# Three elementwise steps of a two-layer graph network on GpSimd in place of VectorE

## The chip, the cores and the metric

The kernel runs on one core of one Trainium2 chip. A core has five engines with a queue each: TensorE (PE, matrix products into PSUM), VectorE (DVE) and ScalarE (ACT, elementwise work), GpSimd (POOL) and SyncE (SP, which here issues almost all DMAs). Each engine works through its own instructions in order and waits on semaphores of the others. The metric is the time of one execution on the device in microseconds; the median of four runs before is 2351.61 us (2350.25 to 2352.42).

## The reference

128 graphs of 128 nodes with 512 features pass through two layers, all in float32. In short:

```python
# x: [128, 128, 512], adj: [128, 128, 128]
h = maximum(layernorm(x), 0)                       # layer 0: a transformer
q, k, v = h @ Wq.T + bq, h @ Wk.T + bk, h @ Wv.T + bv     # 8 heads of 64
s = (q @ k.T) * 64 ** -0.5 * (adj + adj)
x = x + (softmax(s) @ v) @ Wo.T + bo
h = maximum(layernorm(x), 0)                       # layer 1: a graph attention
Wh = h @ W
e = leaky_relu(Wh @ a[:512] + (Wh @ a[512:]).T, 0.2)
att = softmax(where(adj > 0.5, e, -9e15), axis=1)
x = x + elu(att @ Wh)
```

## The kernel before

**Tiling.** The 128 graphs are taken two by two: 64 *pairs* p. Two pairs make a *group* g of four graphs, whose tokens share the q, k and v products. The nodes of a graph lie on the 128 partitions, so the residual x of a pair is a tile `xs[p]` of 128x1024 (two graphs, 512 features). The input transposed, features on partitions, is loaded as the tile `hA` of a group.

**Layer norm of layer 0.** Statistics are taken from rows of x (`stats0`, L165 and L166), the power -1/2 on GpSimd (`row_stats.power`, L172 and L173), and both numbers of each row go through DRAM (`spread0`, a DMA that GpSimd issues at L208; `fetch0`, issued by SP at L213) into a tile `mr` that has them along the free dimension. Then `hidden(p, 0)` (L222) subtracts the means from the pair's half of `hA` and `hidden(p, 1)` (L224) applies the maximum with 0 and multiplies by the scale. These steps are called `hd0` and `hd1`; they exist for pairs 4 to 63. The first four pairs are normalised by rows and turned over by TensorE.

**Products with seven in place of eight.** Each 512x512 product is cut into quarters and done with seven products of quarters (`PRODUCTS`), after sums of quarters have been formed. `token_sum` forms the four sums of an operand: for the hidden rows (`hidden_sum`, steps `hs0` to `hs3`, tile `hS`; the last, L157, overwrites a quarter of `hA`), for the context (`cs`, tile `cxT`) and for the gathered rows of layer 1 (`gs`, tile `gT`). Accumulators lie in eight PSUM banks (`ps1`); a bank is free again when ScalarE or VectorE has read it. The products of the output projection go into `row_a` and `row_c`, and `add0` (L402, steps `od`) adds them to `xs[p]`.

**The constant row.** The biases of v and of the output projection come to one row c that is the same for all tokens. `shift(p)` (L234, step `sh`) adds it to `xs[p]` before the first `od` step of the pair. `xs[p]` has three buffers and is loaded by SP at L72.

**Attention.** TensorE makes scores (L320), VectorE weighs them with the adjacency (L327, `at`) and takes maxima (L334), ScalarE exponentials (L339) and the division (L348). VectorE transposes 32x32 blocks (L355); two DMAs through DRAM place them (L359, L365). TensorE multiplies by v (L388). Layer 1 follows for the pair before: row statistics, `nmr` (L412), hidden rows on ScalarE (L418), dots with a on VectorE (L425), softmax, gathering (L481), the product with W, and the ELU (L511, L515).

**Order.** All of it is written out by hand: the lists `HEAD`, `ORDER` and `TAIL` name steps with the pair they work on, and the program issues them one after another, so that each engine's queue holds its share of them in this order. `ORDER` is one iteration of the steady part, run for p from 3 to 59; with its lags it works on pair p in attention, p-1 in the output projection, p-2 and p-3 in layer 1, and p+4 in the hidden rows. An odd iteration ends with `hs2` and `hs0` of the next group but one; the even iteration after it has `hs1` and `hs3`. GpSimd's queue holds, in each iteration, the power of layer 1 (L172, L173) and that of layer 0 with its DMA (L172, L173, L208).

Of the kernel before, what the change touches and what calls it, by code (L numbers as in the profile page):

```python
# [10 lines left out]
OP = mybir.AluOpType  # L11
AX = mybir.AxisListType

P = 128
# [10 lines left out]
def kernel(  # L25
# [18 lines left out]
    nc = tc.nc  # L44
    B, S, E = x.shape
# [14 lines left out]
    xs, x0s, adjs, adjTs, hAs, hSs = {}, {}, {}, {}, {}, {}  # L60
# [57 lines left out]
    c_sb, u_sb = const.tile([P, E], F32, name="c"), const.tile([P, 2, E], F32, name="u")  # L118
# [26 lines left out]
        else:  # L145
            nc.vector.tensor_tensor(w[:, 6], w[:, 2], w[:, 5], OP.subtract)

    def token_sum(h, s, k):

        if k == 0:  # L150
            nc.vector.tensor_tensor(s[:, 0], h[:, 2], h[:, 3], OP.add)
        elif k == 1:
            nc.vector.tensor_tensor(s[:, 1], s[:, 0], h[:, 0], OP.subtract)  # L153
        elif k == 2:
            nc.vector.tensor_tensor(s[:, 2], h[:, 0], h[:, 2], OP.subtract)
        else:
            nc.vector.tensor_tensor(h[:, 2], h[:, 1], s[:, 1], OP.subtract)  # L157

    def row_stats(src, name, soon=False):

# [56 lines left out]
    def hidden(p, k):  # L217

        h = hAs[p // 2][:, 2 * (p % 2) : 2 * (p % 2) + 2].rearrange("p q c k -> p (q c) k")
        row = rows0[p][:, None, :, k].to_broadcast([P, 2 * 2, 2 * S])  # L220
        if k == 0:
            nc.vector.tensor_tensor(h, h, row, OP.subtract)  # L222
        else:
            nc.vector.scalar_tensor_tensor(h, h, 0.0, row, op0=OP.max, op1=OP.mult)  # L224

    def hidden_sum(g, k):
        if g not in hSs:
            hSs[g] = grp.tile([P, 3, 2, 2 * S], F32, name="hS")
        token_sum(hAs[g], hSs[g], k)

    def shift(p):


        nc.vector.tensor_tensor(xs[p], xs[p], c_sb[:, None, :].to_broadcast([P, 2, E]), OP.add)  # L234

    accs = {}

# [442 lines left out]
    def steps(p):  # L680
# [21 lines left out]
        for k in range(4):  # L702
            table[f"cs{k}"] = lambda k=k: token_sum(cxT, cxT[:, 4:7], k)
            table[f"gs{k}"] = lambda k=k: token_sum(gTs[p], gTs[p][:, 4:7], k)
# [7 lines left out]
        for i in range(2):  # L712
# [9 lines left out]
            "pr": lambda: leaky1(p), "m1": lambda: maxima1(p), "e1": lambda: exps1(p), "sw": lambda: normalise1(p),  # L722
            "ez": lambda: elu(p), "fa": lambda: finish_a(p), "fb": lambda: finish_b(p), "so": lambda: store(p),
            "sh": lambda: shift(p),
        }
        if p < N - 2:
# [18 lines left out]
        if p + 4 < N:  # L745
            table |= {
                "f0": lambda: fetch0(p + 4), "lT": lambda: load_xT(p + 4),
                "hd0": lambda: hidden(p + 4, 0), "hd1": lambda: hidden(p + 4, 1),
            }
# [6 lines left out]
        if odd and (g + 2) * 2 < N:  # L756
            for k in range(4):
                table[f"hs{k}"] = lambda k=k: hidden_sum(g + 2, k)
# [70 lines left out]
```

## Time and profile before

| what | value |
|---|---|
| median of four runs | 2351.61 us |
| the profiled execution | 2352.27 us |
| its span, first to last instruction | 2350.5 us |
| mean granted TensorE clock | 0.997 |
| ScalarE busy | 1467.0 us, 62% |
| GpSimd busy | 256.5 us, 11%, 320 instructions |
| DMA queue of SP (q1) | 311.31 MB, 43.8% of 16 engines' span |

The profile is of one execution. Times in a timeline are microseconds from the span's start. A group of instructions is named by its line in the kernel, its engine, its operation, and out<-in by the program's names with partitions and elements; then come count, busy time, mean length in ns and the idle time of the engine just before, with what ended it. PEld is TensorE's loading of weights, which overlaps its products. A wait names who waited and who released it.

The longest waits of GpSimd and VectorE, in us in total, times, and longest:

```
POOL mv L172 <- DVE mv L166: 1998.0, 123, 34.1
DVE x L402 <- PE row_a L299: 137.1, 149, 2.0
DVE x L234 <- DMA x<-in_x: 40.1, 28, 2.6
DVE at L327 <- PE sc L320: 39.8, 60, 1.2
DVE nmr L412 <- POOL mv L173: 16.8, 28, 0.6
```

### The profile page before, as it was taken

The numbers are of one execution on the slowest core, as the hardware profiler recorded it, in microseconds if no ns is written. First come the engines' busy times: TensorE is split into PE (matmuls) and PEld (weight loads), VectorE is DVE, ScalarE is ACT, GpSimd is POOL, SyncE is SP. The second block draws the span as 40 slices with busy tenths as digits, with TensorE's granted clock in tenths as the row PEclk, the third lists the DMA queues.
The fourth block names the chain that finished last, engine by engine and source line by source line (L and its number), as shares of the span: only waits on it lengthen the run. The fifth ranks groups of instructions, "written<-read, shape, count | busy, mean of one in ns | idle before, by whom it ended". The sixth has DMA issues, their size and how long they took to land.

```text
span 2350.5 us, 41028 instructions
## 1 busy us (share of the span) xinstructions
PE 2336.3 (99%) x14184; PEld 2064.5 (88%) x14184; DVE 2001.5 (85%) x4113; ACT 1467.0 (62%) x4815; POOL 256.5 (11%) x320
## 2 busy tenths in 40 slices
PE   9999999999999999999999999999999999999998
PEld 8888888888888888888888888888888888888886
DVE  5888888888888888888888888888888888888888
ACT  2666566666566665666666666656666566666774
POOL 1101101111111011011110111110101101110000
PEclk8999999999999999999999999999999999999999
DMA  4445354454444544434445445444344443443332
GB/s 157 135 122 148 120 149 117 132 158 127 140 128 126 154 131 137 140 114 145 148 124 152 117 124 161 125 144 136 120 148 136 132 140 112 147 149 118 118 119 95
DMA packets 267351, 314.06 MB, mean 134 GB/s; under 512 B 24200, under 2 KB 192136, under 8 KB 267144
## 3 DMA queue, kind: packets, MB, share of 16 engines
q1 hardware_dynamic: 263112, 311.31, 43.8%
q8 instruction: 112, 1.84, 0.3%
q0 software_dynamic: 1920, 0.13, 0.2%
q14 instruction: 95, 0.78, 0.1%
q10 hardware_dynamic: 2112, 0.01, 0.0%
HBM read 210.51 MB, written 100.85 MB: 132 GB/s over the span
## 4 chain that ended last, share of the span: by engine, by line
PE 99%; DMA 0%; DVE 0%; ACT 0%; issue 0%; SPq 0%; DVEq 0%; ACTq 0%
PE acc_a L258 29%; PE row_a L299 23%; PE acc_c L258 14%; PE row_c L299 9%; PE acc_b L258 7%; PE sc L320 5%; PE pc L388 5%; PE pg L481 5%; DMA wq<-in_wqT 0%; PE pm L531 0%; DMA bq<-in_bq 0%; PE pt L197 0%; ACT z L495 0%; DVE x L402 0%; DVE st L165 0%
## 5 line engine op out<-in xcount | busy, mean ns | idle before, releaser
L339 ACT ACTIVATE at<-at,nmx 128x128 f32<-128x128 f32 x1024 | 396.2, 390 | 19.7 <-DVE nmx L334 17.9
L299 PE MATMUL row_a<-wo,cxT 128*128 128x256 f32 x1280 | 328.5, 379 | 0.3 <-DVE cxT L153 0.3
L348 ACT ACTIVATE at<-at,rs 128x128 f32<-128x128 f32 x1024 | 324.0, 392 | 5.8 <-DVE rs L343 5.7
L299 PE MATMUL row_a<-w,gT 128*128 128x256 f32 x1280 | 319.4, 380 | 2.9 <-DVE z L499 1.7
L172 POOL TENSOR_SCALAR mv<-mv 128x2 f32<-128x2 f32 x124 | 79.2, 638 | 2020.2 <-DVE mv L166 1998.0
L299 PEld LDWEIGHTS row_a<-w,gT 128*128 128x128 f32 x1280 | 242.3, 190 | 37.9 <-DVE z L499 2.6
L299 PEld LDWEIGHTS row_a<-wo,cxT 128*128 128x128 f32 x1280 | 242.6, 190 | 34.3 <-DVE cxT L153 0.6
L402 DVE TENSOR_TENSOR x<-row_a,x 128x256 f32<-128x256 f32 x320 | 135.1, 422 | 139.9 <-PE row_a L299 137.1
L495 ACT COPY z<-row_a 128x256 f32<-128x256 f32 x256 | 94.5, 369 | 210.4 <-PE row_a L299 210.2
L275 ACT ACTIVATE kT<-acc_a,bk 128x256 f32<-128x256 f32 x256 | 106.7, 467 | 171.4 <-PE acc_a L258 168.2
L327 DVE SCALAR_TENSOR_TENSOR at<-sc,adj 128x512 f32<-128x512 f32 x256 | 165.1, 686 | 42.2 <-PE sc L320 39.8
L339 ACT ACTIVATION_READ_ACCUMULATOR at<-at,nmx 128x1 f32 x1024 | 193.7, 189 | 0.0
L275 ACT ACTIVATE qT<-acc_a,bq 128x256 f32<-128x256 f32 x256 | 106.3, 467 | 123.1 <-PE acc_a L258 123.1
L165 DVE BATCH_NORM_STATS2 st<-x 128x6 f32<-128x512 f32 x256 | 176.1, 688 | 7.5 <-DMA x<-in_x 5.2
L425 DVE SCALAR_TENSOR_TENSOR junk<-h,u 128x512 f32<-128x512 f32 x256 | 173.4, 677 | 0.6
L355 DVE STREAM_TRANSPOSE tr<-at 128x1024 f32<-128x1024 f32 x128 | 158.9, 1241 | 9.3 <-PE pc L388 2.7
L334 DVE TENSOR_REDUCE nmx<-at 128x8 f32<-128x1024 f32 x128 | 156.2, 1220 | 4.3
L487 ACT COPY gT<-pg 128x512 f32<-128x512 f32 x128 | 74.7, 585 | 123.6 <-PE pg L481 117.4
L481 PEld LDWEIGHTS pg<-w,h 128*128 128x128 f32 x1024 | 133.3, 192 | 6.6 <-ACT z L495 0.2
L173 POOL TENSOR_TENSOR mv<-mv,mhalf 128x2 f32<-128x2 f32 x128 | 130.6, 1021 | 32.0 <-DVE mv L168 21.7
L481 PE MATMUL pg<-w,h 128*128 128x128 f32 x1024 | 134.1, 275 | 0.0
L299 PE MATMUL row_c<-w,gT 128*128 128x256 f32 x512 | 133.1, 382 | 0.6 <-DVE z L499 0.5
(130 smaller groups left out, 4884.9 us busy)
## 6 DMA issues: line engine op xcount, KB each, us to landing
blocks<-tr SPq DMA_DIRECT2D x128, 512.0 KB, 6.5
aT<-blocks SPq DMA_DIRECT2D x512, 128.0 KB, 2.9
x<-in_x SPq DMA_DIRECT2D x123, 512.0 KB, 5.2
out<-x SPq DMA_DIRECT2D x63, 512.0 KB, 4.1
hA<-in_xT SPq DMA_DIRECT2D x120, 256.0 KB, 3.6
mr<-rows SPq DMA_DIRECT2D x60, 256.0 KB, 4.2
adj<-in_adj SPq DMA_DIRECT2D x64, 128.0 KB, 3.9
adjT<-in_adjT SPq DMA_DIRECT2D x64, 128.0 KB, 3.7
```

Source lines behind the costliest of these rows:

```text
L165: nc.vector.bn_stats(st, src[:, i, :])
L258: nc.tensor.matmul(acc[:, m, :], lhsT, rhs, start=fresh and m == 0 and c == 0, stop=c == 1, skip_group_check=True)
L275: nc.scalar.activation(dst(t, f)[:, m, :], a[:, m, :], AF.Identity, bias=bias[:, j : j + 1])
L299: nc.tensor.matmul(acc, left[:, la, c, :], w[:, wb, c, :], start=n in (0, 3) and c == 0, stop=c == 1, skip_group_check=True)
L327: nc.vector.scalar_tensor_tensor(ats[b][0][:, k * C : (k + 1) * C, :], scs[b][k], QSCALE, adjs[p][:, i : i + 1, :].to_broadcast([P, C, S]) ...
L334: nc.vector.tensor_reduce(nmx, at, AX.X, OP.max, negate=True)
L339: nc.scalar.activation(at[:, j, :], at[:, j, :], AF.Exp, bias=nmx[:, j : j + 1], accum_out=sums[:, j : j + 1])
L348: nc.scalar.activation(at[:, j, :], at[:, j, :], AF.Copy, scale=rs[:, j : j + 1])
L355: nc.vector.transpose(trs[b], at.rearrange("p h (j k) -> p j h k", k=Q))
L402: nc.vector.tensor_tensor(d, row_acc(p, "o", bank), d, OP.add)
L425: nc.vector.scalar_tensor_tensor(junk, h2[:, i, :], 1.0, u_sb[:, k, :], op0=OP.mult, op1=OP.mult, accum_out=ws[:, i, 1:2] if k else src_sb ...
L481: nc.tensor.matmul(pg[:, c, :], h1s[p][0][:, i, c * P : (c + 1) * P], wts[p][:, i, :], start=True, stop=True)
```

## The change

`shift`, the first half of `hidden`, and `token_sum` for the hidden rows of the groups from 2 on are issued to GpSimd. The sums of the first two groups, of the context and of the gathered rows stay on VectorE. The lists of steps are not touched, so the moved instructions stand in GpSimd's queue where the lists have them, between the powers and the small DMAs.

```diff
-    def token_sum(h, s, k):
+    def token_sum(h, s, k, engine=nc.vector):
 
         if k == 0:
-            nc.vector.tensor_tensor(s[:, 0], h[:, 2], h[:, 3], OP.add)
+            engine.tensor_tensor(s[:, 0], h[:, 2], h[:, 3], OP.add)
         elif k == 1:
-            nc.vector.tensor_tensor(s[:, 1], s[:, 0], h[:, 0], OP.subtract)
+            engine.tensor_tensor(s[:, 1], s[:, 0], h[:, 0], OP.subtract)
         elif k == 2:
-            nc.vector.tensor_tensor(s[:, 2], h[:, 0], h[:, 2], OP.subtract)
+            engine.tensor_tensor(s[:, 2], h[:, 0], h[:, 2], OP.subtract)
         else:
-            nc.vector.tensor_tensor(h[:, 2], h[:, 1], s[:, 1], OP.subtract)
+            engine.tensor_tensor(h[:, 2], h[:, 1], s[:, 1], OP.subtract)
...
         if k == 0:
-            nc.vector.tensor_tensor(h, h, row, OP.subtract)
+            nc.gpsimd.tensor_tensor(h, h, row, OP.subtract)
         else:
...
-        token_sum(hAs[g], hSs[g], k)
+        token_sum(hAs[g], hSs[g], k, nc.gpsimd if g > 1 else nc.vector)
 
     def shift(p):
...
-        nc.vector.tensor_tensor(xs[p], xs[p], c_sb[:, None, :].to_broadcast([P, 2, E]), OP.add)
+        nc.gpsimd.tensor_tensor(xs[p], xs[p], c_sb[:, None, :].to_broadcast([P, 2, E]), OP.add)
```

## The prediction, made before the changed kernel was run

> **What bounds the kernel now.** I read the busy times of the page first, then the same by stretches of the span. The columns of a stretch are its length, then busy time and instructions of PE, PEld, DVE, ACT and POOL, the granted clock, the DMA share and GB/s.
>
> ```profile
> PE 2336.3 (99%) x14184; PEld 2064.5 (88%) x14184; DVE 2001.5 (85%) x4113; ACT 1467.0 (62%) x4815; POOL 256.5 (11%) x320
> 90.00:1000.00 910.00, 910.00 (x5541) 805.88 (x5540) 781.07 (x1598) 575.80 (x1900) 99.43 (x122) 1.00 0.45 134
> 1000.00:2260.00 1260.00, 1260.00 (x7721) 1116.72 (x7721) 1081.43 (x2216) 803.71 (x2651) 138.68 (x166) 1.00 0.44 133
> 2260.00:2351.00 91.00, 81.49 (x478) 67.56 (x474) 78.60 (x179) 50.89 (x151) 4.06 (x8) 1.00 0.32 105
> ```
>
> From 90 to 2260 us TensorE has no gap, at full clock. The chain of waits says the same: PE is 99% of it, and its groups return every 72.2 us (an x16 of acc_a at 1023.23, the next at 1095.45). So 233 us of VectorE work can be taken away there without gaining anything; a change can only open gaps. What counts is how late each step may come before PE stands still. I call that its room. 72.2 us are two pairs: an odd iteration (1002 to 1038) and an even one (1038 to 1074).
>
> **What is removed.** VectorE loses these (columns: count | busy us, mean ns | idle before):
>
> ```profile
> L234 DVE TENSOR_TENSOR x<-x,c 128x1024 f32<-128x1024 f32 x64 | 78.2, 1221 | 40.1 <-DMA x<-in_x 40.1
> L222 DVE TENSOR_TENSOR hA<-hA,mr 128x1024 f32<-128x1024 f32 x60 | 73.0, 1216 | 0.0
> L155 DVE TENSOR_TENSOR hS<-hA 128x512 f32<-128x512 f32 x32 | 22.1, 691 | 1.0
> L151 DVE TENSOR_TENSOR hS<-hA 128x512 f32<-128x512 f32 x32 | 21.9, 685 | 1.5 <-ACT hA L200 1.4
> ```
>
> With L153 and L157 (683 and 682 ns) and 30 of each sum moved (the first two groups stay): 78.2 + 73.0 + 30 x (0.691 + 0.685 + 0.683 + 0.682) = 233 us; VectorE falls to about 1768 us, 75%. Worth nothing by itself. No DMA moves, and the orders of PE, ACT and SP are the same.
>
> **What is added.** GpSimd gets 64 + 60 instructions of 1024 elements and 120 of 512. The trace has no elementwise instruction of such length there, so I bound it by its plain ones:
>
> ```profile
> masks.py:199 POOL TENSOR_SCALAR_AFFINE_SELECT ident<-ident 128x128 f32<-128x128 f32 x1 | 0.3, 283 | 0.0
> L371 POOL MEMSET src<- 128x64 f32 x1 | 0.2, 152 | 0.0
> L102 POOL MEMSET mhalf<- 128x1 f32 x1 | 0.1, 98 | 0.0
> ```
>
> Fixed cost 98 ns. Writing alone: (152 - 98)/63 = 0.86 ns an element. Reading one and writing: (283 - 98)/128 = 1.45. Lower end, a second input for nothing: 98 + 1024 x 1.45 = 1.58 us. Upper end, the second input as dear as another pass: 98 + 1024 x 2.9 = 3.07 us. I take one more stream at the write price, 2.31 ns: 2.46 us for 1024, 1.28 us for 512 (bounds 0.84 and 1.58). The sum on GpSimd is 124 x 2.46 + 120 x 1.28 = 459 us (bounds 297 and 570). Even if VectorE stood still through all of it, 1768 + 459 = 2227 us would fit into the span, so VectorE doesn't become the bound on average.
>
> The Trainium skill speaks against the change: GPSIMD Engine Reference, "Performance versus the Vector engine", calls elementwise work with two inputs about twice as slow there and gives 4497 ns against 2293 for 2048 elements. An estimate from that page is 2.25 us for 1024; the sum by it would be 124 x 2.25 + 120 x 1.12 = 413 us, and the rooms below would hold a little more easily.
>
> **What lies in the way of what.** The two engines get into each other's way (timeline: start, length, engine):
>
> ```profile
> 1004.83 1.20 DVE L511 SCALAR_TENSOR_TENSOR x<-z,x 128x1024 f32<-128x1024 f32 x1
> 1005.08 1.02 POOL L172 TENSOR_SCALAR mv<-mv 128x2 f32<-128x2 f32 x1 [22.98 <-DVE mv L166]
> 1016.20 0.30 POOL L172 TENSOR_SCALAR mv<-mv 128x2 f32<-128x2 f32 x1 [8.27 <-DVE mv L166]
> 1016.34 0.42 DVE L499 TENSOR_TENSOR z<-row_a,z 128x256 f32<-128x256 f32 x1
> 1016.58 0.70 POOL L173 TENSOR_TENSOR mv<-mv,mhalf 128x2 f32<-128x2 f32 x1
> ```
>
> L172 takes 0.30 us, but 1.02 when L511 (two inputs in SBUF) runs, and ends 0.07 us after it. L499, with one input in PSUM, leaves L173 at its 0.70. So a VectorE instruction with two SBUF inputs holds GpSimd back until it ends; one that reads PSUM does not. Whether GpSimd holds VectorE back the same way no row shows, for want of long instructions there. Bounds: nothing, or its whole length. I take the whole length, but only against VectorE's two-input instructions. The Trainium skill (SBUF — State Buffer, "SBUF: two separate sides") has it so: the shared port pair is an exclusive lock, and whoever starts first keeps it for the instruction. By it the blocking is the one I take; without it the forecast would lose about 1 us of its tail.
>
> **Shift, even iteration.** The tightest room:
>
> ```profile
> 1060.71 1.23 DVE L234 TENSOR_TENSOR x<-x,c 128x1024 f32<-128x1024 f32 x1 [1.15 <-DMA x<-in_x]
> 1062.47 0.87 DVE L402 TENSOR_TENSOR x<-row_a,x 128x256 f32<-128x256 f32 x2
> 1065.19 1.03 PE L299 MATMUL row_a<-wo,cxT 128*128 128x256 f32 x4
> ```
>
> It starts when x lands, so an early start on another engine wins nothing. On GpSimd it ends at 60.71 + 2.46 = 63.17, L402 twice by 64.1; PE needs that at 1065.0 (its weight load is 0.2 us ahead). 0.9 us are left, and at the upper bound of 3.07 still 0.3. VectorE has nothing with two SBUF inputs to do in that stretch. In two of the later periods (PE at 1859.55 and 2003.97) x landed late enough that VectorE ended only 0.6 and 0.8 us before PE; there PE loses about 0.6 us each: +1.2 us.
>
> **Shift and means, odd iteration.** x is issued at 1015.03, and the transfer is over by about 1018.2 (slices of 0.2 us from 1014, GB/s):
>
> ```profile
> GB/s 0 0 0 0 0 0 0 4 1 0 113 123 0 0 287 420 389 430 389 348 123 0 0 0 5 5 0 0 471 389 410 369 471 287 20 41 20 20 20 20
> 1018.77 1.29 DVE L327 SCALAR_TENSOR_TENSOR at<-sc,adj 128x512 f32<-128x512 f32 x2
> 1019.57 1.08 PE L299 MATMUL row_c<-w,gT 128*128 128x256 f32 x4
> PEld row_c L299 <- DVE at L327: 5.2, 28, 0.2
> ```
>
> GpSimd issues its small DMA until 1018.35, then shifts (18.4 to 20.9) and subtracts the means of a later pair at once (20.9 to 23.3), ten us ahead of before. Beside it VectorE runs L327, which frees a bank for PE with no room at all (the last line: PE waited for it 28 times), but reads PSUM. Then come a maximum (one input) and at 1021.23 four sums with two SBUF inputs, which stand until 1023.3: 2.1 us late, less the 1.2 us of the shift that they no longer wait for. L402 (room 3.3 us to PE at 1028.25) and L279 (3.5 us to 1029.98) come 0.9 us late, and VectorE's idle 2.0 us at 1027.3 takes that up. Nothing reaches PE.
>
> **Sums and the rest.** hs2 and hs0 follow L224 (ends 1036.59) until 1039.2. Queued behind them on GpSimd are the two instructions of the variance (L172 at 1041.09 before), still in time. hs1 follows those and may hold L412 until about 1044.3, against 1043.68 before; the scores that VectorE needs next come at 1044.27. hs1 ends near 1044.3 and PE reads it at 1053.11; hs3 queues behind the small DMA, ends near 1056 and is read at 1061.74. Cover is 5 to 9 us. The means of the even iteration (63.2 to 65.6) are due at 1072.31.
>
> **Head and tail.** The head's moved steps have VectorE consumers 8 us away or more. In the tail, where PE and VectorE alternate without room, the shift at 2299.22 can start earlier but holds three sums (+0.6), and the one at 2313.42 starts when x lands and ends 1.2 us later (+0.7 after an idle 0.4). Sum: 1.2 + 1.3 = +2.5 us.
>
> The profiled execution took 2352.27 us, 2350.5 of it the span; it lies 0.7 us above the median of 2351.61. 2352.27 + 2.5 = 2354.8, or 2354 against the median.
>
> **Rivals.**
> - *GpSimd is too slow (0.22).* Decides from about 3.3 us for 1024 elements: room of the even shift, 1.23 + the 0.4 us that L402 waited for something else + 1.64. Above it each us costs 1 in the even iteration, and from 3.5 us on 2 in the odd one, where shift and means stand in line ahead of the sums. At 4 us: (0.7 + 1.0) x 31 = 53 us, 2405; at 3.6 us 2368. For it: a pow of only two elements takes 0.70 us there, and L172 is stretched threefold by VectorE. Against: the rows of the plain instructions.
> - *GpSimd holds VectorE even where that reads PSUM (0.20).* Then the odd shift, from 18.4 to 20.9, stands on L327 at 1018.77, whose bank PE takes at 1019.57: up to 2.1 us a period, 31 x 2.1 = 65 us, 2417; half as much, 2384, where only one of the pair is caught. It decides as soon as the shift starts before 1018.8. Against: L173 beside L499.
> - *Faster (0.03).* PE's idle 2350.5 - 2336.3 = 14 us lies ahead of 90 and behind 2260; the tail could give back some 5 us if VectorE's lighter queue shortened its alternation: 2346.
> - *It does not do what it says*: excluded, the three lines stand on GpSimd in the built order, 244 of them.
>
> **How the numbers follow.** The forecast, no change to speak of, has 0.55, with a range of its own of 2349 to 2358. What a measurement of this kernel tells from no change is about 0.2%, 4.7 us, so up to 2356.3; of the 0.55 some 0.07 lie above. Same: 0.48. Slower: 0.07 + 0.22 + 0.20 = 0.49. Faster 0.03. The range reaches to 2402: it leaves out about 0.18 in all, most of it the far ends of the two slow rivals.
>
> **What would show it.** Right: the x<-x,c group on POOL at 2.2 to 2.8 us mean, PE without a gap from 90 to 2260, VectorE near 75%, its idle time larger, and the sums at 1021 waiting for POOL. Wrong: POOL means above 3.3 us, PE waits for L402 once in each even iteration, or for L327 in each odd one, longer than 0.2 us; or a period above 72.2 us.

## The result, and the profile after

The changed kernel takes 2354.86 us (median of 42 runs, 2351.37 to 2356.94) against 2351.51 us for the kernel before (60 runs, 2347.8 to 2353.01): a ratio of 1.0016, 95% interval 1.0012 to 1.002. It is about 3.4 us slower, less than the 4.7 us that the prediction took for the limit. The profiled execution took 2354.78 us, 2353.0 of it the span; before it was 2352.27 and 2350.5.

Busy times of the page of the changed kernel, then three stretches of its span (length, then busy us and instructions of PE, PEld, DVE, ACT and POOL, granted clock, DMA share, GB/s):

```profile
PE 2337.4 (99%) x14184; PEld 2064.3 (88%) x14184; DVE 1888.7 (80%) x3869; ACT 1472.5 (63%) x4815; POOL 726.3 (31%) x564
```

```profile
90.00:1000.00 910.00, 910.00 (x5541) 805.81 (x5540) 732.89 (x1494) 578.71 (x1903) 297.49 (x226) 1.00 0.45 134
1000.00:2260.00 1260.00, 1259.74 (x7698) 1115.88 (x7696) 1015.78 (x2079) 806.11 (x2648) 400.56 (x302) 1.00 0.45 133
2260.00:2353.00 93.00, 83.66 (x502) 69.18 (x501) 80.51 (x180) 52.01 (x156) 11.26 (x11) 1.00 0.32 105
```

VectorE has lost 244 instructions and 113 us of busy time, TensorE still has no gap from 90 to 1000 us and only 0.26 us of gaps from there to 2260. The 2.5 us of the span lie ahead of 90, in two spots of the long middle, and in the tail.

The moved groups, and two VectorE groups that were *not* touched by the diff (count | busy us, mean ns | idle before):

```profile
L234 POOL TENSOR_TENSOR x<-x,c 128x1024 f32<-128x1024 f32 x64 | 151.0, 2359 | 204.5 <-DMA x<-in_x 120.5 <-ACT v L270 59.4 <-issue 15.1
L222 POOL TENSOR_TENSOR hA<-hA,mr 128x1024 f32<-128x1024 f32 x60 | 145.0, 2416 | 17.0 <-DMA hA<-in_xT 17.0
...
L157 DVE TENSOR_TENSOR gT<-gT 128x256 f32<-128x256 f32 x64 | 75.3, 1177 | 0.1
...
L412 DVE SCALAR_TENSOR_TENSOR nmr<-mv 128x2 f32<-128x2 f32 x64 | 43.2, 674 | 34.6 <-POOL mv L173 34.6
...
L155 POOL TENSOR_TENSOR hS<-hA 128x512 f32<-128x512 f32 x30 | 38.3, 1277 | 377.5 <-DVE hA L224 377.5
L151 POOL TENSOR_TENSOR hS<-hA 128x512 f32<-128x512 f32 x30 | 38.1, 1269 | 14.9 <-DVE hA L224 14.9
```

The first two rows and the last two are the price: 2.36 and 2.42 us for 1024 elements, 1.26 to 1.29 us for 512. The middle two are the news. In the profile before the same groups were these:

```profile
L157 DVE TENSOR_TENSOR gT<-gT 128x256 f32<-128x256 f32 x64 | 26.6, 416 | 0.1
...
L412 DVE SCALAR_TENSOR_TENSOR nmr<-mv 128x2 f32<-128x2 f32 x64 | 10.0, 156 | 16.8 <-POOL mv L173 16.8
```

L412 handles two numbers a partition, yet its mean went from 156 to 674 ns. The timeline says how (start, length, engine). First an odd iteration of the changed kernel, then the even one after it:

```profile
1019.83 1.29 DVE L327 SCALAR_TENSOR_TENSOR at<-sc,adj 128x512 f32<-128x512 f32 x2
1019.96 2.35 POOL L234 TENSOR_TENSOR x<-x,c 128x1024 f32<-128x1024 f32 x1 [0.55 <-DMA x<-in_x]
...
1020.63 1.08 PE L299 MATMUL row_c<-w,gT 128*128 128x256 f32 x4
...
1022.28 2.39 POOL L222 TENSOR_TENSOR hA<-hA,mr 128x1024 f32<-128x1024 f32 x1
1022.29 2.65 DVE L157 TENSOR_TENSOR gT<-gT 128x256 f32<-128x256 f32 x1
...
1044.24 1.26 POOL L153 TENSOR_TENSOR hS<-hS,hA 128x512 f32<-128x512 f32 x1
1044.30 1.22 DVE L412 SCALAR_TENSOR_TENSOR nmr<-mv 128x2 f32<-128x2 f32 x1 [0.61 <-POOL mv L173]
...
1062.01 2.35 POOL L234 TENSOR_TENSOR x<-x,c 128x1024 f32<-128x1024 f32 x1 [5.30 <-DMA x<-in_x]
...
1064.39 0.88 DVE L402 TENSOR_TENSOR x<-row_a,x 128x256 f32<-128x256 f32 x2 [0.77 <-POOL x L234]
...
1066.26 1.03 PE L299 MATMUL row_a<-wo,cxT 128*128 128x256 f32 x4
```

L327 runs beside the shift in its usual 1.29 us, and PE takes its bank. L157, 0.42 us long before, is drawn out to 2.65 us: it starts with L222 and ends 0.27 us after it. L412 is drawn out to 1.22 us and ends 0.02 us after L153. So a held VectorE instruction doesn't show as idle time; its record is as long as the hold. The whole trace says the same: of the VectorE instructions that begin while a moved instruction runs on GpSimd with more than 0.3 us to go, all 63 with two inputs in SBUF are drawn out and end 0.01 to 0.55 us after it, and none of the 425 others, which have one input or read PSUM, is longer than before by as much as 0.1 us. The busy time of VectorE in the new page is its work and 103 us of standing still (what 64 records are longer than before), which makes the work about 1786 us. The prediction's 1768 took the moved records off in full, though neighbouring records overlap by a little under 0.1 us. In the even iteration the shift ends at 1064.36, L402 at 1065.27, and PE comes at 1066.26 with its weight load 0.2 us ahead: 0.8 us of room are left. Over 28 even iterations, from 195 to 2151 us, this room is 0.05 to 1.12 us and 0.66 on average, since x lands at a different time in each.

Three rows of the list of what TensorE itself waited for, in the changed kernel (us in total, times, longest):

```profile
PE acc_b L258 <- DVE at L327: 1.3, 1, 1.3
PE row_a L299 <- DVE cxT L153: 0.8, 1, 0.8
...
PE row_a L299 <- DVE x L402: 0.2, 1, 0.2
```

The first and the last did not stand in the list before, and the middle one stood there with 0.3 us. The first is in the head, where the chain led through a sum of weights (L144, 0.68 us long before, started at 61.48):

```profile
61.01 3.13 DVE L144 TENSOR_TENSOR wo<-wo 128x512 f32<-128x512 f32 x1
61.23 2.36 POOL L234 TENSOR_TENSOR x<-x,c 128x1024 f32<-128x1024 f32 x1
...
67.81 1.28 DVE L327 SCALAR_TENSOR_TENSOR at<-sc,adj 128x512 f32<-128x512 f32 x2
...
68.54 0.70 PE L258 MATMUL acc_b<-hA,wk 128*128 128x256 f32 x2 [1.27 <-DVE at L327]
```

The shift of pair 0 stood in VectorE's queue behind other work before and started at 70.18. On GpSimd's empty queue it starts nine microseconds sooner, and L144, which has two inputs in SBUF, stands still until it is over. L327 came at 65.82 before and comes at 67.81 now. Three lines of the profile before:

```profile
61.48 0.68 DVE L144 TENSOR_TENSOR wo<-wo 128x512 f32<-128x512 f32 x1
...
67.58 1.89 PE L258 MATMUL acc_b<-hA,wk 128*128 128x256 f32 x8
...
70.18 1.22 DVE L234 TENSOR_TENSOR x<-x,c 128x1024 f32<-128x1024 f32 x1
```

The second is in the tail (its row of waits names cxT, which comes late because of it):

```profile
2314.30 0.86 POOL L173 TENSOR_TENSOR mv<-mv,mhalf 128x2 f32<-128x2 f32 x1
2315.14 2.35 POOL L234 TENSOR_TENSOR x<-x,c 128x1024 f32<-128x1024 f32 x1
...
2315.20 2.31 DVE L412 SCALAR_TENSOR_TENSOR nmr<-mv 128x2 f32<-128x2 f32 x1 [0.17 <-POOL mv L173]
```

In the profile before:

```profile
2313.34 0.16 DVE L412 SCALAR_TENSOR_TENSOR nmr<-mv 128x2 f32<-128x2 f32 x1 [0.17 <-POOL mv L173]
2313.42 1.23 DVE L234 TENSOR_TENSOR x<-x,c 128x1024 f32<-128x1024 f32 x1
```

L412 took 0.16 us there before and was *ahead* of the shift in VectorE's queue; now the shift starts 0.06 us sooner than L412 and holds it until 2317.51, and the hidden rows on ScalarE and all that follows them come later. That is no accident of timing. L412 waits for L173, and the shift stands directly behind L173 in GpSimd's queue, with no wait between the two. In all 30 holds of L412 in this trace the instruction that holds it is the one directly behind L173, and it begins 0.06 us ahead.

Comparing the start of every TensorE product in the two traces gives the account of the span: 0.5 us earlier at the start, +1.5 at 67.6 us, +0.8 in the middle (two even iterations at 2004 and 2148, where x landed late), +1.4 from 2317 to 2319, and the span ends 0.75 us sooner after its last product: -0.5 + 1.5 + 0.8 + 1.4 - 0.75 = 2.5 us. The three losses alone are 3.7 us, near the 3.35 us by which the medians differ. At 2148 the chain shows why x was late: its load (3.99 us) follows the storing of an earlier pair (`out<-x`, 7.69 us) at once.

### The profile page after: what moved, and what is told of

It is laid out like the page before. It is cut to its first block, busy times and chain, and to the rows that moved or that the text cites. A ratio compares the mean times of both kernels' runs of the same rounds, so it can differ in the third digit from the quotient of the medians.

```text
span 2353.0 us, 41178 instructions
## 1 busy us (share of the span) xinstructions
PE 2337.4 (99%) x14184; PEld 2064.3 (88%) x14184; DVE 1888.7 (80%) x3869; ACT 1472.5 (63%) x4815; POOL 726.3 (31%) x564
## 4 chain that ended last, share of the span: by engine, by line
PE 97%; DVE 2%; DMA 1%; POOL 0%; ACT 0%; issue 0%; SPq 0%; POOLq 0%; DVEq 0%; ACTq 0%
PE acc_a L258 28%; PE row_a L299 23%; PE acc_c L258 14%; PE row_c L299 9%; PE acc_b L258 7%; PE sc L320 5%; PE pc L388 5%; PE pg L481 5%; DMA x<-in_x 1%; DMA out<-x 0%; DVE st L165 0%; POOL x L234 0%; PE pt L197 0%; DVE x L402 0%; PE pm L531 0%; DVE nmr L412 0%
## 5 line engine op out<-in xcount | busy, mean ns | idle before, releaser
L348 ACT ACTIVATE at<-at,rs 128x128 f32<-128x128 f32 x1024 | 328.8, 391 | 45.1 <-DVE rs L343 45.0
L402 DVE TENSOR_TENSOR x<-row_a,x 128x256 f32<-128x256 f32 x320 | 134.3, 420 | 195.3 <-PE row_a L299 167.5
L234 POOL TENSOR_TENSOR x<-x,c 128x1024 f32<-128x1024 f32 x64 | 151.0, 2359 | 204.5 <-DMA x<-in_x 120.5
L327 DVE SCALAR_TENSOR_TENSOR at<-sc,adj 128x512 f32<-128x512 f32 x256 | 164.7, 684 | 29.9 <-PE sc L320 27.4
L173 POOL TENSOR_TENSOR mv<-mv,mhalf 128x2 f32<-128x2 f32 x128 | 151.7, 1185 | 31.1 <-DVE mv L168 20.8
L155 POOL TENSOR_TENSOR hS<-hA 128x512 f32<-128x512 f32 x30 | 38.3, 1277 | 377.5 <-DVE hA L224 377.5
L222 POOL TENSOR_TENSOR hA<-hA,mr 128x1024 f32<-128x1024 f32 x60 | 145.0, 2416 | 17.0 <-DMA hA<-in_xT 17.0
```

Source lines behind the costliest of these rows:

```text
L173: nc.gpsimd.tensor_tensor(mv[:, :, 1], mv[:, :, 1], mhalf.to_broadcast([P, 2]), OP.pow)
L234: nc.gpsimd.tensor_tensor(xs[p], xs[p], c_sb[:, None, :].to_broadcast([P, 2, E]), OP.add)
L327: nc.vector.scalar_tensor_tensor(ats[b][0][:, k * C : (k + 1) * C, :], scs[b][k], QSCALE, adjs[p][:, i : i + 1, :].to_broadcast([P, C, S]) ...
L348: nc.scalar.activation(at[:, j, :], at[:, j, :], AF.Copy, scale=rs[:, j : j + 1])
```

## The experiments

**The two ends on VectorE.** If the losses in head and tail come from the shifts of pairs 0 and 63, giving these two back to VectorE must remove them. Two kernels, against the changed one:

```diff
-        nc.gpsimd.tensor_tensor(xs[p], ...
+        (nc.vector if p == 0 else nc.gpsimd).tensor_tensor(xs[p], ...           # first_v
+        (nc.vector if p in (0, N - 1) else nc.gpsimd).tensor_tensor(xs[p], ...  # ends_v
```

> Only the shift of pair 0 goes back to VectorE. Theory (three spots): the constant row's first addition, which on GpSimd starts at 61.2 us and holds a two-input sum of weights (L144) for 3.1 us, is worth 1.3 us of PE's wait at 67.6; without it PE stands there as before, and the time falls by 1.3 us, to about 2353.6. Rival (diffuse contention in every iteration, the 1.3 us at the head being a chance of that one execution): PE's wait at the head comes and goes by itself, the time stays at 2354.9.

> The shifts of pair 0 and of pair 63 go back to VectorE. Theory: both the 1.3 us at the head and the 1.5 us at the tail (L412 held for 2.3 us) are gone; what is left is the late landings of x in even iterations, 0.3 to 0.8 us: about 2352.2, within 0.04% of before. Rival (diffuse): at least 2354.

Measured: 2353.18 us with pair 0 back (11 runs; ratio to before 1.001, 1.0001 to 1.0019), 2352.07 with both (11 runs; 1.000, 0.9992 to 1.0009), against 2351.53 before (33 runs). By the medians pair 0 was worth 1.7 us and pair 63 another 1.1, and with both gone no loss can be measured; the intervals of neighbouring kernels overlap, so the split rests on the trace. The jump of TensorE's starts at 67.6 us is gone in both traces.

**The two ends alone on GpSimd.** The converse: the kernel before, and only these two of the 244 instructions moved.

```diff
-        nc.vector.tensor_tensor(xs[p], ...
+        (nc.gpsimd if p in (0, N - 1) else nc.vector).tensor_tensor(xs[p], ...
```

> The kernel before, with the shift of pairs 0 and 63 alone on GpSimd; the other 62 shifts, the means and the sums stay on VectorE. Theory (at the two ends the shift on GpSimd holds a VectorE instruction with two inputs in SBUF that stands on the way to TensorE, L144 in the head and L412 in the tail): it has both losses of the changed kernel and none of its others, 1.3 + 1.5 = 2.8 us, about 2354.3; L144 near 3.1 us long in place of 0.68 and L412 near 2.3 in place of 0.16. Rival (the losses at the two ends come from the queue of GpSimd as the whole change fills it, or from VectorE's changed order of work): without the rest of the change they are gone, 2351.6 to 2352.

Measured: 2354.8 us (11 runs) against 2352.15 (15 runs), ratio 1.0011, 1.0002 to 1.002. Two instructions cost 2.65 us, close to both losses in the changed kernel together (1.5 + 1.4). The interval is wide, 0.5 to 4.7 us, so the size rests on the trace. The timeline of this kernel:

```profile
60.59 3.15 DVE L144 TENSOR_TENSOR wo<-wo 128x512 f32<-128x512 f32 x1
60.81 2.37 POOL L234 TENSOR_TENSOR x<-x,c 128x1024 f32<-128x1024 f32 x1
...
2313.88 2.34 POOL L234 TENSOR_TENSOR x<-x,c 128x1024 f32<-128x1024 f32 x1
2313.94 2.30 DVE L412 SCALAR_TENSOR_TENSOR nmr<-mv 128x2 f32<-128x2 f32 x1 [0.18 <-POOL mv L173]
```

Both holds are there with the rest of the kernel untouched, and TensorE's starts jump by 1.5 us at 67.6 and by 1.4 at 2317 to 2319. The rival, a fuller GpSimd queue or VectorE's altered order, falls.

**Shift alone, and the rest alone.** Each half of the change by itself: `shift_only` has the means and sums back on VectorE, `rest_only` the shift.

```diff
-            nc.gpsimd.tensor_tensor(h, h, row, OP.subtract)                     # shift_only
+            nc.vector.tensor_tensor(h, h, row, OP.subtract)
...
-        token_sum(hAs[g], hSs[g], k, nc.gpsimd if g > 1 else nc.vector)         # shift_only
+        token_sum(hAs[g], hSs[g], k)
...
-        nc.gpsimd.tensor_tensor(xs[p], ...                                      # rest_only
+        nc.vector.tensor_tensor(xs[p], ...
```

> Only the shift is on GpSimd; means and sums of the hidden rows are on VectorE. Theory: all three spots belong to the shift, so the whole difference stays: 2354.9, if not a little more, since VectorE is busier in even iterations. Rival (the cost is that of the amount of work on GpSimd, 151 of 449 us): a third of the difference, 2352.6.

> The shift is on VectorE; means and sums of the hidden rows are on GpSimd. Theory: no gap opens in PE between 90 and 2260 us and none at the ends: 2351.5, as before, though 155 us of VectorE are free. Rival (amount of work): two thirds of the difference, 2353.7.

Measured: `shift_only` 2356.43 us (11 runs; ratio 1.0019, 1.001 to 1.0027), `rest_only` 2352.24 (11 runs; 1.0001, 0.9992 to 1.0011), against the same 2351.53. The whole loss goes with the shift; 180 of the 244 moved instructions cost nothing that can be told. That `shift_only` is 1.6 us above the whole change is partly a matter of its executions: in the profiled one TensorE ran at a granted clock of 0.57 in a stretch of 4 us near the end, where the profile after has full clock, and 1.5 us were lost there.

```profile
2335.00:2339.00 4.00, 4.00 (x12) 3.21 (x12) 1.89 (x8) 1.84 (x7) 0.00 (x0) 0.57 0.00 0
```

In how many of its other runs this happened isn't known; three of the eleven took 2353.7 to 2353.9 us at a mean clock of 0.998, the others 2355.7 to 2357.9 at 0.996 or 0.997. Without that loss its last product stands 2.9 us later than before, the changed kernel's 3.3.

`rest_only` has a hold of its own, with a price:

```profile
2163.48 2.39 POOL L222 TENSOR_TENSOR hA<-hA,mr 128x1024 f32<-128x1024 f32 x1
2163.54 2.35 DVE L412 SCALAR_TENSOR_TENSOR nmr<-mv 128x2 f32<-128x2 f32 x1 [0.62 <-POOL mv L173]
2165.81 1.28 DVE L327 SCALAR_TENSOR_TENSOR at<-sc,adj 128x512 f32<-128x512 f32 x2
...
2166.54 0.85 PEld L388 LDWEIGHTS pc<-aT,v 128*64 128x64 f32 x16 [0.32 <-DVE at L327]
```

Here it is the subtraction of means that starts 0.06 us ahead of L412, L327 begins 1.4 us later than at 2164.42 before, and TensorE's starts slip by 1.2 us between 2160 and 2260. In the changed kernel the same L412 takes 0.16 us: there the shift stands between L173 and L222 in GpSimd's queue, and it waits for x until 2175.34. In the steady part of each of the two kernels L153 on GpSimd holds L412 29 times (31 us in sum) with no loss to TensorE. So a hold can cost more than half of its length or nothing, by the room behind it.

**The rooms.** The prediction's forecast rests on rooms of 0.9 us in the even iteration and over 3 us in the odd one. To test them GpSimd adds zeros to a half, or to the whole, of x ahead of the shift of pairs 3 to 59; the added instruction leaves the values as they are.

```diff
+    zero = const.tile([P, 1], F32, name="zero")
+    nc.gpsimd.memset(zero, 0.0)
...
+        if 3 <= p < N - 4:
+            d = xs[p][:, 0:1, :]      # late_half; in late_full [:, 0:2, :], and [P, 2, E] below
+            nc.gpsimd.tensor_tensor(d, d, zero[:, None, :].to_broadcast([P, 1, E]), OP.add)
```

> Pairs 3 to 59: ahead of the shift GpSimd adds a column of zeros to half of x (512 elements, 1.27 us), so the result of the shift comes 1.27 us later; no other change in what is computed. Theory (rooms): in the even iteration L402 ends 0.8 us before PE needs it, so PE stands 0.5 us in each of 29 of them, +14 us; in the odd iteration the room is 2.3 us, no loss: about 2369. Rival (cost by the amount of GpSimd's work, 3.4 us for 449): 72 us more of it cost 0.6 us, 2355.5.

> The same with all of x (1024 elements, 2.36 us later). Theory (rooms): even iterations lose 2.36 - 0.8 = 1.6 us each, 29 of them, 46 us; odd ones have 2.3 us of room at L402 and less on the way over ScalarE to kT, some 0.2 us each: about 2405. Rival (amount of work): 2356.

Measured: 2368.15 us (4 runs; ratio 1.0077, 1.0062 to 1.0092) and 2389.94 (4 runs; 1.0173, 1.0156 to 1.019), against 2351.65 (7 runs). One even iteration of the second (its lines lie five lower: L239 is the shift, L407 the addition of the projection, L304 the product):

```profile
1074.67 1.89 POOL L238 TENSOR_TENSOR x<-x,zero 128x1024 f32<-128x1024 f32 x1 [5.06 <-DMA x<-in_x]
...
1076.64 2.35 POOL L239 TENSOR_TENSOR x<-x,c 128x1024 f32<-128x1024 f32 x1
...
1079.03 0.88 DVE L407 TENSOR_TENSOR x<-row_a,x 128x256 f32<-128x256 f32 x2 [2.51 <-POOL x L239]
...
1079.97 1.13 PE L304 MATMUL row_a<-wo,cxT 128*128 128x256 f32 x4 [0.64 <-DVE x L407]
```

The added instruction takes 1.89 us, 1.97 with the gap behind it (1076.64 - 1074.67); less the mean room of 0.66 that is 1.31 us in an even iteration, and 28 x 1.31 = 37 us. Measured were 35.1 us over the changed kernel. In the list of waits this is one row:

```profile
PE row_a L304 <- DVE x L407: 28.7, 29, 1.5
```

Its 28.7 us are less than what was lost: it counts from the ends of products, which the profile models. By the starts of products 28 even iterations lost 0.8 to 1.7 us each, 35.0 in sum (the 29th, that of pair 59, lost nothing), and one odd iteration lost 1.6. The forecast of 2405 was too high for two reasons that the trace shows: the instruction took 1.89 us in place of the 2.36 supposed, and a loss of 0.2 us in each odd iteration came in none but that one.

That odd iteration had been near the edge in the changed kernel already:

```profile
877.85 0.42 DVE L157 TENSOR_TENSOR gT<-gT 128x256 f32<-128x256 f32 x1
877.88 2.60 POOL L234 TENSOR_TENSOR x<-x,c 128x1024 f32<-128x1024 f32 x1 [2.91 <-DMA x<-in_x]
```

x landed late there. L157 got ahead, and the shift was drawn out to 2.60 us; then the shift held the next sum and L222 the one after it, 2.58 and 2.60 us. L402 ended 0.18 us before TensorE's weight load, where the other odd iterations have 2.1 us and more.

Of half of x, the time is within 1 us of the forecast, though by another sum. The added instruction takes 1.04 us and x comes 1.12 later: 0.46 us over the mean room, 12.9 us in 28 iterations; 13.3 us were measured over the changed kernel. Most iterations lost 0.1 to 0.7 us, two with a late landing 1.6 and 1.4. So the even room is real, is about 0.7 us on average, and each microsecond past it costs about one.

## Why the prediction was right, and which of its terms were not

**The middle was right.** The forecast was that 2.46 us in place of 1.22 fits into every room between 90 and 2260, and that VectorE's relief is worth nothing. The instruction took 2.36 to 2.42, 113 us less of VectorE busy time gained nothing, and the period stayed at 72.2 us. In the odd iteration L402 came 0.9 us later, as forecast: 3.3 us ahead of TensorE before, 2.3 to 2.4 in most iterations after. The two kernels with a later x show that the room of the even iteration ends near where the prediction put it: it read 0.9 us off one iteration, and the changed kernel has 0.8 there and 0.66 on average. It is no single figure: 0.05 us was the least.

**The price was right by its way of counting.** One stream more at the price of a write gave 2.46 and 1.28 us; measured 2.36 to 2.42 and 1.26 to 1.29. The estimate from the Trainium skill (GPSIMD Engine Reference, "Performance versus the Vector engine"), 2.25 and 1.12 us, was 5 to 13% low.

**The hold was right in kind, and this case now shows it in both directions.** In all 30 holds of L412 in the changed kernel, 29 by L153 and one by the shift in the tail, it ends 0.015 to 0.022 us after the GpSimd instruction beside it. The Trainium skill (SBUF — State Buffer, "SBUF: two separate sides") calls the shared port an exclusive lock; L157 at 2.65 us and L412 at 2.31 agree with it. That whoever starts first keeps it can't be read off the recorded starts: L144 was recorded 0.22 us ahead of the shift and was held all the same. One of the prediction's signs missed for the same cause: VectorE was to be near 75% with more idle time, and it is at 80%, because its standing still is recorded as work. Instructions that read PSUM are not held, and that settles the second rival: none of the 256 records of L327 in the changed kernel is longer than 0.69 us, and in the tail of the changed kernel L327 starts 0.05 us after the shift of pair 62 and takes its 1.29 us for two.

```profile
2296.53 2.37 POOL L234 TENSOR_TENSOR x<-x,c 128x1024 f32<-128x1024 f32 x1 [9.48 <-DVE tr L355]
2296.58 1.29 DVE L327 SCALAR_TENSOR_TENSOR at<-sc,adj 128x512 f32<-128x512 f32 x2
```

The first rival needed 3.3 us an instruction and got 2.36; `late_full` shows what it would have cost. Of the third, a faster tail, nothing was seen.

**The sum was right by luck of its terms.** It said +2.5 us and the profiled execution shows 2.5 (the medians 3.35), but no term was the size it had:

| term | predicted | measured |
|---|---|---|
| head | 0 | 1.5 |
| two even iterations with a late x | 1.2 | 0.8 |
| tail, shift of pair 62 | 0.6 | 0 |
| tail, shift of pair 63 | 0.7 | 1.4 |
| start of the span, and from the last product to its end | not in the sum | -1.2 |

The two even iterations are not the two that the prediction named. It had those at 1859.55 and 2003.97; in the changed kernel the first lost nothing, the second 0.35 us, and a third at 2148.40 lost 0.44.

The step that failed is "The head's moved steps have VectorE consumers 8 us away or more". It asked who waits for the moved instruction, and not whom it holds. By its own rule of the hold it should have asked that at every place where the shift can start earlier than before. The tail had both questions, and there the first shift came early enough to end (2298.90) just before the three sums (2299.03), and the second stood in front of L412, not in front of a consumer of x: the price was what the chain could not take up of a hold of 2.15 us, not the extra 1.2 us of the shift's own length. That this shift "starts when x lands" was a misreading: before, it followed L412 with no wait for x, and in the changed kernel it follows L173.

## What to carry to other kernels

Moving work to an engine with an empty queue makes it start earlier as well as last longer; with GpSimd and VectorE ask of each moved instruction not only who waits for its result but which VectorE instruction with both inputs in SBUF will start within its length, and how much room lies behind that one. Look first at a moved instruction directly behind a GpSimd instruction whose result VectorE waits for: here it went ahead of the waiting one every time. A hold was free where TensorE had work queued and cost 1.2 to 1.5 us out of 2.2 to 2.5 where the room behind it was short, so a change that is neutral in the steady part can be decided by two instructions out of 244 at the ends. And where a kernel is bound by another engine without a gap, relief of VectorE buys nothing: 180 moved instructions changed the time by less than can be measured.

## What the runs showed of the hardware that was not expected

- A VectorE instruction that GpSimd holds is recorded as a long instruction, not as idle time (L412 0.16 to 2.31 us, L144 0.68 to 3.13). The record's start doesn't say who has the port: L144 is recorded 0.22 us ahead of the shift and was held all the same.
- GpSimd's addition is quicker when one operand is a single column repeated: 1.04 us for 512 elements and 1.89 for 1024, against 1.26 to 1.29 and 2.36 with two full operands.
- Near the start of the span TensorE runs in some stretches at about half its clock, and how long differs from execution to execution. From 40 to 44 us the granted clock was 0.57 in the profiled execution before, with 12 products; in `late_full`, whose products there are the same, it was 1.00 with 20.

```profile
40.00:44.00 4.00, 4.00 (x12) 3.23 (x11) 3.85 (x9) 0.00 (x0) 2.41 (x3) 0.57 0.39 134
```

```profile
40.00:44.00 4.00, 4.00 (x20) 3.51 (x20) 2.32 (x5) 0.00 (x0) 1.26 (x2) 1.00 0.34 125
```

That shifted whole executions against the one before by 1.7 us (`first_v`, `ends_v`, `ends_only`, `shift_only`, `late_half`) to 3.3 us (`late_full`) between 30 and 66 us. Differences of a microsecond between single executions of this kernel are therefore read from the starts of products at one place, not from the time alone.
